# Layer 2's attention: scores ahead of two down products of layer 1, interleaved output products at its end, roots as powers, softmax weights shared by two engines

## The chip, the cores and the metric

The kernel runs on one core of one Trainium2 chip. The metric is the device time of one execution in microseconds (us). Engines: PE (TensorE: matmuls and transposes), DVE (VectorE), ACT (ScalarE), POOL (GpSimd), and SP (SyncE), which only issues DMAs. Each engine runs its instructions in a fixed order; what it needs from another engine it waits for.

## The reference

A model of four layers works on a residual x of 4 x 256 tokens by 256 features. Each layer adds a gated cross-attention over 64 context tokens per batch row, and then a gated feed-forward part; both read the layer-normalised x:

```
for n in 0..3:
    x = x + tanh(g_xattn[n]) * attention_n(layernorm(x), ctx)
    x = x + tanh(g_ffn[n])   * ffn_n(layernorm(x))
layernorm(x) = (x - mean) / sqrt(var + 1e-5)
```

Layers 0 and 1 have a latent attention with 16 heads; layers 2 and 3 a plain one with 16 heads of 16 features and a causal mask (scores = q k / 4, softmax, times v, output product). The feed-forward parts: 0 is a mixture of 16 experts (6 per token) with a shared one, 1 is an MLP 256-1024-256 with weights quantised to -1, 0, 1, 2 is a linear layer with row-wise rounding to 8 bits of both sides, 3 is a mixture of 8 experts (2 per token) with a shared one.

## The kernel before, in words

The 1024 tokens are 8 tiles of 128 (NT = 8), in two groups of four (g = 0, 1; TPG = 4). The residual `x[t]` stays in SBUF. A Python program writes the steps in an order, and a scheduler of the framework orders each engine's instructions from it; `behind(a, b)` adds an edge that keeps a after b on their engines without a wait, `tc.high_priority` pulls a step ahead.

**Softmax attention by tiles.** `in_flight` (L519) runs a pipeline over the tiles: in step i the scores of tile i, the gated add into x of tile i-3, the softmax weights of tile i-1, and `attend` of tile i-2. The scores of a tile go to a `wide` PSUM tile (two exist), DVE takes the row maximum (L1090 in layers 2 and 3, L482 in 0 and 1) and subtracts it (L1092, L483), ACT takes the exponential (L1101, L484). `weights` (L486): DVE sums (L490) and inverts (L491), POOL multiplies all 128x1024 values (L492). `attend` in layers 2 and 3 (L1104): PE transposes the weights (`transposed_pairs`, L506), ACT copies them out of PSUM in two halves (L507), PE multiplies by the values (L1109), ACT copies the context (`ctxTok`, L1118), PE makes the output product (L1121); DVE adds it to x, times the gate (`gated_add`, L517). In layers 0 and 1 `attend` is one product (L714). PSUM has four more `mm` buffers, which all other products share in turn.

**Around layer 2.** `ffn1` (L1886) ends with eight down products (`down`, L1916), each of 24 matmuls on a tile, an addition of the bias and a gated add on DVE. Among the last four stand layer 2's key and value steps (`keys_values`, L1000 and L1016), the layer norm of group 0, its transposes (L461) and its queries (`head_queries`, L476 and L1034). All eight come before the scores of layer 2. Then `used` frees the weight slot of the down products, and SP issues four late loads of layer 3 (L231 and L330).

In layer 2 a side step runs in each step of the pipeline: `queries(1)` (L1043: layer norm of group 1, transposes, queries), and `beside2` (L1130), which makes layer 3's keys and values and at the end calls `rounded(0)` (L1995): layer norm of group 0 for the feed-forward part of layer 2, rounded to whole numbers. `ffn2` (L2016) turns these on PE (L2025), multiplies (L2034), adds (DVE L2038, POOL L2039), rounds group 1, and prepares layer 3's first queries; `kept_busy` (L510) puts matmuls without use there (L512).

**Layer norm** (`layernorm`, L425): DVE's statistics of four tiles (L430, L433), ACT's root (L435, with a load of ACT's table when another function was there), DVE's reciprocal (L438), for the `scalar` form a shift (L442), then four normalised tiles by DVE (L449) or ACT (L446).

Of the kernel before, what the change touches and what calls it, by code (L numbers as in the profile page):

```python
# [30 lines left out]
F32 = mybir.dt.float32  # L31
# [4 lines left out]
AF = mybir.ActivationFunctionType  # L36
# [3 lines left out]
P = 128  # L40
# [57 lines left out]
def tile_flamingo(ctx: ExitStack, tc: tile.TileContext, a: dict, out: bass.AP):  # L98
# [88 lines left out]
    eps = const.tile([P, 1], F32, tag="eps", name="eps")  # L187
    nc.gpsimd.memset(eps, EPS)
    root = small([P, 1], "root", 1)
    nc.scalar.activation(root, eps, AF.Sqrt)  # L190
# [233 lines left out]

    def layernorm(g, scalar=False, after=()):  # L425

        mv = small([P, TPG, 2], "mv")
        for i in range(TPG):
            st = small([P, 6], "st")
            made = nc.vector.bn_stats(st, x[g * TPG + i])  # L430
            if after:
                behind(made, after[0])
            nc.vector.bn_aggr(mv[:, i, :], st)  # L433
        rstd = small([P, TPG], "rstd")
        made = nc.scalar.activation(rstd, mv[:, :, 1], AF.Sqrt, bias=eps)  # L435
        if after:
            behind(made, after[1])
        nc.vector.reciprocal(rstd, rstd)  # L438
        xn = []
        if scalar:  # L440
            shift = small([P, TPG], "shift")
            nc.vector.scalar_tensor_tensor(shift, mv[:, :, 0], -1.0, rstd, ALU.mult, ALU.mult)  # L442
# [42 lines left out]

    def weights(e):  # L486

        groups, n = e.shape[1], e.shape[2]
        sm = sb.tile([P, 16], F32, tag="sm", name="sm", bufs=3)[:, :groups]
        nc.vector.tensor_reduce(sm, e, AX.X, ALU.add)  # L490
        nc.vector.reciprocal(sm, sm)  # L491
        nc.gpsimd.tensor_tensor(e, e, sm.unsqueeze(2).to_broadcast([P, groups, n]), ALU.mult)  # L492

# [24 lines left out]

    def in_flight(scores, attend, gate, beside=iter(())):  # L519

        made, outs = {}, {}
        for i in range(NT + 3):
# [5 lines left out]
            if 1 <= i <= NT:  # L528
                weights(made[i - 1])
            if 2 <= i < NT + 2:  # L530
                outs[i - 2] = attend(i - 2, made.pop(i - 2))

    def paired(steps):
# [143 lines left out]
    def latent_attend(products, wvo, gate, swapped=False, beside=iter(())):  # L677
# [38 lines left out]

        in_flight(scores, attend, gate, beside)

# [318 lines left out]
    def attention23(layer, gate, beside):  # L1037
# [5 lines left out]
        def queries(g):  # L1043

            xn = layernorm(g, layer == 3)
            yield
            xT = transposed(xn)
            yield
            qT.append(head_queries(layer, xT))
# [7 lines left out]
        def scores(t):  # L1057
# [24 lines left out]

            last = side_by_side(lambda half=half, a=a: part(half, a) for half in range(2) for a in range(2))
            if layer == 3 and t == 2:
# [6 lines left out]
            for a in range(2):  # L1091
# [8 lines left out]
                )  # L1100
            nc.scalar.activation(e, e, AF.Exp)  # L1101
            return e

        def attend(t, e):  # L1104
            aT = transposed_pairs(e)
            ps = ps_mm()
# [10 lines left out]
            cT = sb.tile([P, 2 * P], F32, tag="xn", name="ctxTok", bufs=AHEAD + 2)  # L1117
            nc.scalar.copy(cT, ps[:, : 2 * P])  # L1118
            ps = ps_mm()
# [5 lines left out]

        in_flight(scores, attend, gate, zip_longest(queries(1), beside))
        if layer == 3:
            used("L3")

    def beside2(keys):  # L1130
        for i in range(NT + 3):
            if i == NT + 1:
                kept["rounded"] = rounded(0)
            next(keys, None)
            yield
# [750 lines left out]
    def ffn1(gate):  # L1886
# [28 lines left out]

        def down(g, i, terms):  # L1916
            ps = ps_mm()
            for f in range(8):
                for k in range(3):
                    nc.tensor.matmul(  # L1920
                        ps[:, :D],
# [3 lines left out]
                        stop=(f == 7 and k == 2),  # L1925
                    )
            y = sb.tile([P, D], F32, tag="xn", name="y", bufs=AHEAD + 2)
            nc.vector.tensor_tensor(y, ps[:, :D], b2_1, ALU.add)
            gated_add(g * TPG + i, y, gate)

        terms = [up(g) for g in range(NG)]
# [276 lines left out]
```

## Time and profile before

| | us |
|---|---|
| median of 3 runs | 826.48 (822.49 to 829.31) |
| profiled execution, its own time | 826.97 |
| its span in the trace | 825.1 |
| mean granted clock of PE | 0.991 |
| attention of layer 0, 149 to 207: PE busy | 53.91 of 58 |
| attention of layer 1, 420 to 487: PE busy | 64.52 of 67 |
| last up and all down products, 505 to 539: PE busy | 33.95 of 34 |
| attention and feed-forward of layer 2, 539 to 603: PE busy | 55.52 of 64 |
| attention of layer 3, 603 to 653: PE busy | 43.93 of 50 |

All places in time are us from the start of the span. A timeline line has start, length, engine, line, operation, output<-input, shapes and count, and in brackets the idle time of the engine before it with the engine and line that ended it. An fp32 matmul of the program appears as two in the trace. A digit of the page's slices is the busy share in tenths; PEclk is the clock that was granted to PE, 1.00 or 9 being full.

### The profile page before, as it was taken

The numbers are of one execution on the slowest core, as the hardware profiler recorded it, in microseconds if no ns is written. First come the engines' busy times: TensorE is split into PE (matmuls) and PEld (weight loads), VectorE is DVE, ScalarE is ACT, GpSimd is POOL, SyncE is SP. The second block draws the span as 40 slices with busy tenths as digits, with TensorE's granted clock in tenths as the row PEclk, the third lists the DMA queues.
The fourth block names the chain that finished last, engine by engine and source line by source line (L and its number), as shares of the span: only waits on it lengthen the run. The fifth ranks groups of instructions, "written<-read, shape, count | busy, mean of one in ns | idle before, by whom it ended". The sixth has DMA issues, their size and how long they took to land. (4 is left out here: it accounts for less than half of the span.)

```text
span 825.1 us, 12510 instructions
## 1 busy us (share of the span) xinstructions
PE 779.1 (94%) x4509; PEld 523.8 (63%) x4512; DVE 496.2 (60%) x1146; ACT 291.5 (35%) x508; POOL 245.9 (30%) x211
## 2 busy tenths in 40 slices
PE   6999999899999899999999999998898899999994
PEld 4544433777565677766656565755445656999993
DVE  4664455775594455543868759889779564334331
ACT  2221111443421333331643468266455421233320
POOL 0454544232113244322021110024424103444332
PEclk9999999999999999999999999999999999999998
DMA  9510114710021253333840001540000102232211
GB/s 340 198 39 1 39 58 160 274 38 26 26 67 48 63 125 68 73 78 77 296 156 1 8 1 33 191 166 1 26 1 2 52 9 78 53 49 44 29 16 18
DMA packets 32467, 62.44 MB, mean 76 GB/s; under 512 B 5552, under 2 KB 19504, under 8 KB 31696
## 3 DMA queue, kind: packets, MB, share of 16 engines
q1 hardware_dynamic: 25008, 51.91, 18.4%
q0 software_dynamic: 7104, 9.41, 6.8%
q8 instruction: 39, 0.64, 0.3%
q10 hardware_dynamic: 288, 0.26, 0.1%
q14 instruction: 28, 0.23, 0.1%
HBM read 52.81 MB, written 9.27 MB: 75 GB/s over the span
## 5 line engine op out<-in xcount | busy, mean ns | idle before, releaser
L492 POOL TENSOR_TENSOR attn<-attn,sm 128x1024 f32<-128x1024 f32 x32 | 61.1, 1911 | 217.9 <-DVE sm L491 169.1
L476 PE MATMUL wide<-xT,big 128*128 128x512 f32 (+1 forms) x240 | 108.7, 600 | 1.1 <-DVE shared L1678 0.9
L742 DVE TENSOR_TENSOR rope<-wide,big 128x512 f32<-128x512 f32 x96 | 59.6, 682 | 52.1 <-PE wide L476 52.1
L476 PEld LDWEIGHTS wide<-xT,big 128*128 128x128 f32 (+1 forms) x240 | 43.7, 189 | 57.3 <-issue 49.2
L1451 PE MATMUL wide<-blk,still 128*128 128x128 f32 x640 | 74.8, 275 | 0.6 <-DVE blk L1423 0.6
L1451 PEld LDWEIGHTS wide<-blk,still 128*128 128x128 f32 x640 | 73.1, 192 | 0.8 <-issue 0.8
L714 PE MATMUL mm<-vo,attnT 128*128 128x256 f32 x256 | 58.6, 382 | 1.5 <-ACT attnT L507 1.5
L476 PE MATMUL wide<-xT,dense 128*128 128x512 f32 (+1 forms) x120 | 55.1, 599 | 0.0
L714 PEld LDWEIGHTS mm<-vo,attnT 128*128 128x128 f32 x256 | 47.8, 190 | 11.4 <-ACT attnT L507 3.3
L507 ACT COPY attnT<-mm 128x512 f32<-128x512 f32 x64 | 34.6, 587 | 45.6 <-PE mm L506 45.1
L490 DVE TENSOR_REDUCE sm<-attn 128x16 f32<-128x1024 f32 x32 | 38.7, 1208 | 15.2 <-ACT attn L484 13.8
L1413 DVE COPY still<-big 128x1024 f32 x20 | 13.9, 693 | 52.1 <-PE wide L1451 44.7
L1485 POOL DMA_INDIRECT out_dram<-ring,scratch x20 | 31.5, 1577 | 39.3 <-DVE ring L1478 15.7
L1485 POOL DMA_INDIRECT sums<-ring,big x17 | 26.9, 1584 | 48.4 <-ACT ring L1567 18.8
L506 PE MATMUL mm<-ident,attn 128*128 128x128 f32 x256 | 35.4, 284 | 4.5 <-POOL attn L492 4.5
L1469 PE MATMUL mm<-big,hidden 128*128 x160 | 37.8, 380 | 1.4 <-DVE hidden L1462 1.4
L1386 POOL DMA_INDIRECT xs<-xd,scratch x20 | 20.0, 999 | 63.2 <-PE mm L1420 36.7
L506 PEld LDWEIGHTS mm<-ident,attn 128*128 128x128 f32 x256 | 30.6, 146 | 12.6 <-POOL attn L492 7.7
L1461 ACT ACTIVATE hidden<-wide 128x512 f32<-128x512 f32 x20 | 11.9, 597 | 71.2 <-PE wide L1451 66.1
L476 PEld LDWEIGHTS wide<-xT,dense 128*128 128x128 f32 (+1 forms) x120 | 21.5, 185 | 24.4 <-issue 22.0
L517 DVE SCALAR_TENSOR_TENSOR x<-mm,tg,x 128x256 f32<-128x256 f32 x44 | 20.4, 469 | 26.9 <-PE mm L714 15.0
L750 POOL TENSOR_TENSOR rotated<-rope 128x512 f32<-128x512 f32 x12 | 15.3, 1271 | 58.6 <-DVE rope L742 58.6
(363 smaller groups left out, 1572.2 us busy)
## 6 DMA issues: line engine op xcount, KB each, us to landing
big<-in_L_w_gate_up SPq DMA_DIRECT2D x8, 1024.0 KB, 10.4
big<-in_L_w_down SPq DMA_DIRECT2D x8, 512.0 KB, 11.0
w_L_qk<-in_L_qk SPq DMA_DIRECT2D x4, 896.0 KB, 9.5
big<-in_L_w SPq DMA_DIRECT2D x2, 1480.0 KB, 8.1
big<-in_L_w SPq DMA_DIRECT2D x2, 1110.0 KB, 5.2
big<-in_L_wo SPq DMA_DIRECT2D x1, 2048.0 KB, 15.0
big<-in_L_w SPq DMA_DIRECT2D x2, 1024.0 KB, 5.4
xd<-xn SPq DMA_DIRECT2D x16, 128.0 KB, 1.8
```

What stands on the lines that cost most here:

```text
L476: nc.tensor.matmul(ps, w(c), xT[:, c, :], start=(c == 0), stop=(c == 1))
L490: nc.vector.tensor_reduce(sm, e, AX.X, ALU.add)
L492: nc.gpsimd.tensor_tensor(e, e, sm.unsqueeze(2).to_broadcast([P, groups, n]), ALU.mult)
L506: nc.tensor.transpose(ps[:, i * P : (i + 1) * P], ev[:, pr * P : (pr + 1) * P], ident)
L507: nc.scalar.copy(aT[:, half * 4 : half * 4 + 4, :].rearrange("p i t -> p (i t)"), ps)
L517: return nc.vector.scalar_tensor_tensor(x[t], ps, gate, x[t], ALU.mult, ALU.add)
L714: nc.tensor.matmul(ps[:, :D], aT[:, s, :], vo[:, s, :], start=(s == 0), stop=(s == NP - 1))
L742: nc.vector.tensor_tensor(m[:, s, :].rearrange("q (b t) -> q b t", t=S), ps[:, s, :].rearrange("q (b t) -> q b t", t=S), table, ALU.mult,)
L1386: nc.gpsimd.indirect_dma_start(out=xs, out_offset=None, in_=self.xd, in_offset=bass.IndirectOffsetOnAxis(ap=self.gather[:, b : b + 1].bitc ...
L1451: made = nc.tensor.matmul(ps[:, k, f : f + P], w[:, at : at + P], st[:, c * P : (c + 1) * P], start=(c == 0), stop=(c == 1),)
L1469: made = nc.tensor.matmul(ps[:, :D], hT[:, j * P : (j + 1) * P], self.w[:, bass.ds(r + j * D, D)], start=(j == 0), stop=(j == n - 1),)
L1485: nc.gpsimd.indirect_dma_start(out=self.sums[b % len(self.sums)], out_offset=bass.IndirectOffsetOnAxis(ap=self.scatter[:, b : b + 1].bitca ...
```

## The change

1. `ffn1` makes six of its eight down products, then layer 2's first queries. The last two, `down(1, 2)` and `down(1, 3)`, become a generator `down_2`, which stands ahead of `queries(1)` in the side steps of layer 2's pipeline; each of their matmuls is put behind the last scores made so far. With them moves what frees their weights and issues layer 3's late loads.
2. Layers 2 and 3 use `in_flight_parts`: `attend` is cut into transposes, `context` and `output`; for the last tiles the output product of a tile stands after the transposes of the next, and before its values.
3. `layernorm(..., powered=True)` makes 1/root as a power: an addition on DVE and a power (-0.5) on POOL. It is used in layer 2 for group 1's queries and for both groups of `rounded`. `beside2` makes the layer norm one step before the rounding.
4. `weights(e, shared=True)`: DVE multiplies the first eight heads, POOL the last eight. Layers 2 and 3: last tile. Layers 0 and 1: tiles 0, 6 and 7.

```diff
+    power = const.tile([P, 1], F32, tag="power", name="power")
+    nc.gpsimd.memset(power, -0.5)
...
-    def layernorm(g, scalar=False, after=()):
+    def layernorm(g, scalar=False, after=(), powered=False):
...
-        made = nc.scalar.activation(rstd, mv[:, :, 1], AF.Sqrt, bias=eps)
-        if after:
-            behind(made, after[1])
-        nc.vector.reciprocal(rstd, rstd)
+        if powered:
+            nc.vector.tensor_scalar_add(rstd, mv[:, :, 1], EPS)
+            nc.gpsimd.tensor_tensor(rstd, rstd, power.to_broadcast([P, TPG]), ALU.pow)
+        else:
+            made = nc.scalar.activation(rstd, mv[:, :, 1], AF.Sqrt, bias=eps)
+            if after:
+                behind(made, after[1])
+            nc.vector.reciprocal(rstd, rstd)
...
-    def weights(e):
+    def weights(e, shared=False):
...
-        nc.vector.reciprocal(sm, sm)
-        nc.gpsimd.tensor_tensor(e, e, sm.unsqueeze(2).to_broadcast([P, groups, n]), ALU.mult)
+        made = nc.vector.reciprocal(sm, sm)
+        parts = [(nc.vector, slice(0, groups // 2)), (nc.gpsimd, slice(groups // 2, groups))]
+        for engine, part in parts if shared else [(nc.gpsimd, slice(0, groups))]:
+            one = e[:, part]
+            engine.tensor_tensor(one, one, sm[:, part].unsqueeze(2).to_broadcast(list(one.shape)), ALU.mult)
+        return made
...
+    def in_flight_parts(scores, turn, context, output, gate, beside):
+
+        made, ctx, outs = {}, {}, {}
+
+        def add(t):
+            outs[t] = output(ctx.pop(t))
+
+        for i in range(NT + 4):
+            next(beside, None)
+            if i < NT:
+                made[i] = scores(i)
+            if i >= 3 and i - 3 in outs:
+                gated_add(i - 3, outs.pop(i - 3)[:, :D], gate)
+            if 1 <= i <= NT:
+                sums = weights(made[i - 1], shared=i == NT)
+            t = i - 2
+            if 0 <= t < NT:
+                aT = turn(made.pop(t))
+            if t >= NT - 2:
+                add(t - 1)
+                made_x = gated_add(t - 1, outs.pop(t - 1)[:, :D], gate)
+                if t == NT - 2:
+                    behind(made_x, sums)
+            if 0 <= t < NT:
+                ctx[t] = context(t, aT)
+            if 0 <= t < NT - 3:
+                add(t)
+            if t == NT:
+                break
...
-        in_flight(scores, attend, gate, beside)
+        in_flight(scores, attend, gate, beside, shared=(0, NT - 2, NT - 1))
...
-            xn = layernorm(g, layer == 3)
+            xn = layernorm(g, layer == 3, powered=(layer == 2))
...
-        def attend(t, e):
-            aT = transposed_pairs(e)
+        def context(t, aT):
...
-            nc.scalar.copy(cT, ps[:, : 2 * P])
+            made = nc.scalar.copy(cT, ps[:, : 2 * P])
+            if t == NT - 3:
+                behind(made, kept["exp"])
+            return cT
+
+        def output(cT):
...
-        in_flight(scores, attend, gate, zip_longest(queries(1), beside))
+        in_flight_parts(scores, transposed_pairs, context, output, gate, zip_longest(chain(kept.pop("others", ()), queries(1)), beside))
...
+            if i == NT:
+                xn = layernorm(0, True, powered=True)
             if i == NT + 1:
-                kept["rounded"] = rounded(0)
+                kept["rounded"] = rounded(0, xn)
...
+        def down_2():
+            yield
+            down(1, 2, terms[1], kept["scored"])
+            yield
+            down(1, 3, terms[1], kept["scored"])
+            used("L1_w2")
+            load_experts3(EARLY3, E3)
...
         down(1, 0, terms[1])
+        xn = layernorm(0)
         next(keys)
-        xn = layernorm(0)
         down(1, 1, terms[1])
-        next(keys)
-        down(1, 2, terms[1])
+        xT_2 = transposed(xn)
         for _ in range(2):
             next(keys)
-        down(1, 3, terms[1])
-        xT_2 = transposed(xn)
+        kept[2, 0] = head_queries(2, xT_2)
         for _ in keys:
             pass
-        kept[2, 0] = head_queries(2, xT_2)
-        used("L1_w2")
-        load_experts3(EARLY3, E3)
+        kept["others"] = down_2()
...
-    def rounded(g):
+    def rounded(g, xn=None):
...
-        xn = layernorm(g, True)
+        xn = xn or layernorm(g, True, powered=True)
```

More of the change, by code (lines that the diff above doesn't have):

```diff
@@ L517, in gated_add, with in_flight @@
         return nc.vector.scalar_tensor_tensor(x[t], ps, gate, x[t], ALU.mult, ALU.add)
-    def in_flight(scores, attend, gate, beside=iter(())):
+    def in_flight(scores, attend, gate, beside=iter(()), shared=()):
         made, outs = {}, {}
@@ L528, in in_flight @@
             if 1 <= i <= NT:
-                weights(made[i - 1])
+                weights(made[i - 1], shared=i - 1 in shared)
             if 2 <= i < NT + 2:
                 outs[i - 2] = attend(i - 2, made.pop(i - 2))
+    def in_flight_parts(scores, turn, context, output, gate, beside):
[24 more added lines that the diff above has]
+                break
     def paired(steps):
@@ L1081, in part @@
                 )
-            last = side_by_side(lambda half=half, a=a: part(half, a) for half in range(2) for a in range(2))
+            kept["scored"] = last = side_by_side(lambda half=half, a=a: part(half, a) for half in range(2) for a in range(2))
             if layer == 3 and t == 2:
@@ L1100, in scores @@
                 )
-            nc.scalar.activation(e, e, AF.Exp)
+            kept["exp"] = nc.scalar.activation(e, e, AF.Exp)
             return e
-        def attend(t, e):
-            aT = transposed_pairs(e)
+        def context(t, aT):
             ps = ps_mm()
@@ L1914, in up, with down @@
             return hidden[:, g]
-        def down(g, i, terms):
+        def down(g, i, terms, after=None):
             ps = ps_mm()
@@ L1919, in down @@
                 for k in range(3):
-                    nc.tensor.matmul(
+                    made = nc.tensor.matmul(
                         ps[:, :D],
@@ L1926, in down @@
                     )
+                    if after is not None:
+                        behind(made, after)
             y = sb.tile([P, D], F32, tag="xn", name="y", bufs=AHEAD + 2)
```

## The prediction

> **What bounds the kernel now.** I read the page's busy shares first, then stretches of layer 2, then the timelines of PE and DVE there.
>
> ```profile
> PE 779.1 (94%) x4509; PEld 523.8 (63%) x4512; DVE 496.2 (60%) x1146; ACT 291.5 (35%) x508; POOL 245.9 (30%) x211
> ...
> PE   6999999899999899999999999998898899999994
> ...
> PEclk9999999999999999999999999999999999999998
> ```
>
> PE is the bound (94%), so time is won only where PE sits idle or slow. Stretches (columns: length, then busy PE, PEld, DVE, ACT, POOL, granted clock, DMA share):
>
> ```profile
> 523.00:539.00 16.00, 16.00 (x102) 11.02 (x102) 12.67 (x39) 2.62 (x8) 0.00 (x0) 1.00 0.69 244
> 539.00:550.00 11.00, 10.03 (x50) 5.33 (x50) 9.28 (x12) 8.46 (x15) 2.24 (x2) 1.00 0.61 238
> 550.00:560.00 10.00, 9.51 (x84) 5.95 (x82) 9.46 (x15) 5.91 (x11) 3.73 (x3) 1.00 0.01 2
> 560.00:570.00 10.00, 9.43 (x79) 5.89 (x78) 9.69 (x16) 6.29 (x13) 5.34 (x5) 1.00 0.00 0
> 570.00:580.00 10.00, 7.57 (x61) 4.88 (x60) 7.36 (x20) 5.83 (x11) 4.18 (x4) 0.91 0.01 2
> 580.00:590.00 10.00, 7.39 (x67) 5.01 (x66) 6.84 (x23) 5.66 (x12) 2.78 (x4) 0.92 0.06 8
> ```
>
> Until 539 PE is full (down products). From 540 to 570 DVE is full with softmax. From 570 to 588 neither is: PE goes tile by tile through transposes, copy, values, copy, output. PE's timeline of that end, with the idle time before each piece in brackets:
>
> ```profile
> 573.62 1.13 PE L1121 MATMUL mm<-w_L,ctxTok 128*128 128x256 f32 x4 [0.49 <-ACT ctxTok L1118]
> 574.58 1.04 PE L506 MATMUL mm<-ident,attn 128*128 128x128 f32 x8
> 576.65 0.91 PE L1109 MATMUL mm<-attnT,values 128*32 128x128 f32 x16 [1.03 <-ACT attnT L507]
> 578.06 2.02 PE L1121 MATMUL mm<-w_L,ctxTok 128*128 128x256 f32 x4 [0.49 <-ACT ctxTok L1118]
> 579.87 1.86 PE L506 MATMUL mm<-ident,attn 128*128 128x128 f32 x8
> ```
>
> The last two took 2.02 and 1.86 us for 1.13 and 1.04: the granted clock was about half for 3.4 us, after a stretch (574.5 to 578.0) in which PE was busy 1.97 of 3.5 us. Layer 0 shows the same at its first tile, and an idle piece at its last but one:
>
> ```profile
> 155.36 1.97 PE L506 MATMUL mm<-ident,attn 128*128 128x128 f32 x8 [1.65 <-POOL attn L492]
> ...
> 197.62 1.09 PE L506 MATMUL mm<-ident,attn 128*128 128x128 f32 x8 [0.98 <-POOL attn L492]
> ```
>
> DVE's timeline gives its marks; the last line is a 128x4 operation with two SBUF inputs that takes 0.16 us elsewhere and here ends with the POOL weights (576.53 to 578.43):
>
> ```profile
> 540.48 1.22 DVE L1090 TENSOR_REDUCE mx<-wide 128x16 f32<-128x1024 f32 x1 [2.27 <-PE wide L1075]
> ...
> 574.62 1.22 DVE L490 TENSOR_REDUCE sm<-attn 128x16 f32<-128x1024 f32 x1 [1.18 <-ACT attn L1101]
> ...
> 576.65 1.80 DVE L442 SCALAR_TENSOR_TENSOR shift<-mv,rstd 128x4 f32<-128x4 f32 x1
> ```
>
> **The change, part by part.** I placed the new order of each engine by hand, with spacings of the profiled rows: 8 transposes 1.02, scores 1.07, one key half or value step 0.63, head queries 3.63, a down product 2.72, values 0.67 to 0.92, output 1.05; on DVE row maximum 1.15, subtraction 1.20, row sum 1.13, gated add 0.40; on ACT exponential 1.05, two copies 1.05; POOL weights 1.90.
>
> *Scores ahead of the down products.* Both orders agree to 526.27. Then: transposes 1.0, key half 0.6, value 0.55, head queries 3.63, three values 1.6, scores 1.07, in all 8.5: scores of tile 0 are done at 534.75 (before: 540.4). The two moved products (5.44 of PE, the same work) now cover the softmax of tiles 0 and 1. Gain for DVE at this place: 5.7.
>
> *What is late next.* Group 1's queries need the last down product, now done at 541.85 (before 533.4). Behind it stand on DVE its addition, a sum and a maximum; then the new root and xn, done at 549.05 (before 538.2). On PE, transposes of xn and tile 1, its values and output stand ahead of the head queries, and wait for copies (0.85, 1.2): queries 555.65 to 559.3, scores of tile 4 at 561.0 (before 557.75). DVE, 5.7 ahead at the start, stands idle 4.0 there. From that maximum on it has 15.4 left to the last row sum, which starts at 576.5, 1.9 later than before. The early start by itself buys nothing at this point.
>
> *Interleaved products.* The tail was not bound by that sum: its weights were ready at 578.43 and used at 584.30. In the new order transposes of tile 6 wait for their weights (576.1 to 578.0), then output 5, values 6, transposes 7, output 6, values 7, output 7: 1.0 + 1.05 + 0.65 + 1.0 + 0.55 (copy behind the four xn on ACT) + 1.05 + 0.65 + 0.45 + 1.05 = 7.45, so 585.5 instead of 588.35. The copies' waits (0.49 twice, 0.3 to 0.4 twice) lie under other products and the 1.7 of slow clock and the table load (1.28 on ACT, 0.7 of PE's 1.03) fall away. Through layer 2's feed-forward the chain last gated add, statistics, shift follows: shift at 589.1 instead of 592.21. Gain 3.0; ends 0 (queries 3 later still) and 5.7 (DVE keeps its lead). The four y there (1.66 on DVE) hide its power. Two order-only edges (context copy 5 behind the last exponential, gated add 5 behind the last row sum's reciprocal) are in these times: the copy is ready 2 us after that exponential, and nothing but statistics follows the add.
>
> *Roots as powers.* Three times a 128x4 addition on DVE (0.2) and a power on POOL replace root (0.30), reciprocal (0.18) and one table load. No row shows a power. Ends: 0.19 (a 128x8 cast on POOL) and 1.90 (POOL's weights); I take 0.5, near the small row. It stands ahead of POOL's weights of tiles 1 and 7, and DVE's xn waits for it; both are in the times above. The constant -0.5 is one memset of 0.09 beside the first loads: nothing.
>
> *Weights shared.* Half on POOL: 1.05 (between 0.40 for 128x128 and 1.91 for 128x1024); half on DVE: 0.69 (128x512 from SBUF twice). If they overlap, a tile's weights are 0.85 shorter; if they exclude each other, 0.17. The 1.80 above, and another 128x512 operation of 1.73 instead of 0.48 beside POOL's weights at 452, speak for exclusion; subtraction from PSUM beside POOL keeps its 1.28. The Trainium skill, SBUF — State Buffer, "Who interferes with whom", states it: a DVE instruction with two SBUF inputs contends with a GpSimd one that reads SBUF, and the loser blocks. By that rule the sum stands as below; by free overlap it would be 1.4 lower. I take exclusion. It counts where PE waits for POOL: layer 0, tiles 0 and 6 (2 x 0.15), plus 0.46 of layer 0's scores that now stand ahead of tile 0's transposes in that idle time: 0.8. Ends: 0 (DVE's copy delayed by 0.7 to 1.2, covered by its own wait of 1.51 at 159.45) and 3.2 (overlap twice, and no slow clock at 155.36). Layer 1: PE waited 0.30 there; its DVE halves lie before waits of 2.5: 0 (ends -0.3 and 0.3). Layer 2 and 3's tile 7: not waited for.
>
> *Layer 3.* Same interleaving: outputs 5 and 6 lose 0.49 each, values 6 and 7 0.29 each, less 0.3 for tile 6's weights (POOL 641.82 to 643.72): gain 1.2 (ends 0.3, 1.6).
>
> *Queues.* SP issues the four last loads (533.51 on) some 8 us later; they land in about 10 and are first read at 653: nothing.
>
> Sum: 0.8 + 3.0 + 1.2 = 5.0. Profiled execution 826.97 (span 825.1): 822.0; it stands 0.5 over the median 826.48, so **821.5**.
>
> **The rivals.**
> - *Clock falls at group 1's queries.* In my placing PE is busy about 1.7 of 3.5 us before them; 1.97 of 3.5 was followed by half clock, 2.65 (571.0 to 574.5) was not. 3.4 us at half clock cost 1.7: 823.2. Against it: three estimated waits make that idle. The Trainium skill, TensorE: Matmul & The Clock Gate, Part 1, ties the drop to an idle window of about 3.4 us; by it there would be none. The trace dropped after gaps of only 1.03 and 1.65.
> - *Overlap and kept clock in layer 0.* Gain there 3.2 instead of 0.8, and up to 2 us less waiting at the queries: 816 to 819. For it: POOL's row alone sets T0's wait. Against it: the 1.80.
> - *The late queries take everything.* Layer 2's gain 0 if they come 3 us later still: 824.5.
> - *Slower: the power is slow.* With a price p it delays xn of group 1 and, ahead of tile 7's weights, the tail (0.25 of slack): loss 2p - 1.2. At 1.9 us: 824; from 3.1 us the change is slower than before, at 5 us 830. No POOL row that computes is over 1.9, but none is a power.
>
> **How the numbers follow.** Forecast 0.45, clock falls 0.17, overlap 0.25, late queries 0.08, slow power 0.05. A measurement of this kernel tells about 1% (8.3 us) from none: faster by over 1% is below 818.2. That holds 0.18 of the overlap case and 0.07 of the forecast's edge: 0.25. Slower by over 1% (834.7): half of the slow power and a little, 0.04. Rest 0.71. The range 815.5 to 827 leaves out 0.1 below and 0.1 above.
>
> **What would show it.** Scores of tile 0 about 5.5 us earlier than before; DVE idle some 4 us ahead of tile 4's maximum; the last output 2 to 4 us earlier, with no wait for the context copy before outputs 5 and 6; the power below 1 us; DVE's half of the weights starting when POOL's ends. I am wrong if the power is over 2 us, if DVE does not stand at tile 4, or if PE's clock falls in a new place.

## The result, and the profile after

The changed kernel takes 827.86 us (median, 825.13 to 831.33) beside 825.3 (822.32 to 829.31) before: a ratio of 1.004, 95% interval 1.0025 to 1.0055. It is 0.4% slower, about 2.6 us, where 5 us less was forecast. The profiled execution took 827.87 (span 826.0). A second measurement of the same kernel, later, gave 827.23 and a ratio of 1.0024 (1.0005 to 1.0043).

The first lines of the page, as shown of before:

```profile
PE 777.5 (94%) x4509; PEld 523.2 (63%) x4512; DVE 505.3 (61%) x1154; ACT 290.8 (35%) x505; POOL 244.0 (30%) x215
...
PEclk9999999999999999999999999999999999999998
```

The shares tell nothing; only DVE has 9 us more work. The stretches of layer 2 (length, busy PE, PEld, DVE, ACT, POOL, granted clock, DMA share, GB/s):

```profile
539.00:550.00 11.00, 8.03 (x66) 5.18 (x64) 10.47 (x15) 4.10 (x9) 4.65 (x3) 1.00 0.77 267
550.00:560.00 10.00, 8.15 (x44) 5.15 (x45) 9.23 (x19) 4.44 (x8) 2.58 (x3) 0.83 0.34 127
560.00:570.00 10.00, 10.00 (x67) 5.80 (x66) 6.19 (x9) 4.14 (x9) 1.41 (x1) 1.00 0.00 0
570.00:580.00 10.00, 8.19 (x72) 5.17 (x70) 8.91 (x17) 7.21 (x14) 4.18 (x6) 1.00 0.01 2
580.00:590.00 10.00, 7.49 (x83) 5.25 (x84) 8.79 (x30) 5.84 (x13) 6.65 (x7) 1.00 0.01 2
```

From 539 to 560 PE is busy 16.18 us of 21, where it was 19.54, and from 550 to 560 its clock was 0.83, not 1.00. From 560 to 570 DVE is busy 6.19 of 10 us, where it was full. The clock of 0.91 and 0.92 that was granted from 570 to 590 is gone. PE's timeline there, with idle time in brackets:

```profile
547.32 1.13 PE L1165 MATMUL mm<-w_L,ctxTok 128*128 128x256 f32 x4 [0.49 <-ACT ctxTok L1157]
550.49 1.64 PE L467 MATMUL mm<-ident,xn 128*128 128x128 f32 x8 [2.04 <-DVE xn L455]
...
553.61 1.94 PE L516 MATMUL mm<-ident,attn 128*128 128x128 f32 x8 [0.86 <-ACT xT L169]
...
558.52 3.60 PE L482 MATMUL mm<-xT,w_L 128*128 128x512 f32 x8
...
581.90 1.09 PE L516 MATMUL mm<-ident,attn 128*128 128x128 f32 x8 [0.70 <-POOL attn L501]
```

The transposes of group 1's xn wait 2.04 us and again inside (1.64 for 1.02, since xn is done at 551.3); tile 1's wait 0.86 and then run at about half clock (1.94 for 1.09), which lasts from 553.1 to 556.5. The queries are at 558.52. Before, they and the scores of tile 4, the first that need them, were here:

```profile
542.87 3.70 PE L476 MATMUL mm<-xT,w_L 128*128 128x512 f32 x8
...
552.92 1.14 PE L1075 MATMUL wide<-kbd,xT 64*128 64x256 f32 x8
```

DVE's timeline shows why xn was late:

```profile
542.28 2.04 DVE L527 SCALAR_TENSOR_TENSOR x<-y,tg,x 128x256 f32<-128x256 f32 x1
...
548.34 2.97 DVE L455 TENSOR_SCALAR xn<-x,mv,rstd 128x256 f32<-128x256 f32 x4 [0.46 <-POOL rstd L439]
...
563.66 1.22 DVE L1130 TENSOR_REDUCE mx<-wide 128x16 f32<-128x1024 f32 x1 [3.73 <-PE wide L1115]
...
580.07 1.20 DVE L496 TENSOR_REDUCE sm<-attn 128x16 f32<-128x1024 f32 x1
```

And POOL's, in the same stretch:

```profile
542.14 1.90 POOL L501 TENSOR_TENSOR attn<-attn,sm 128x1024 f32<-128x1024 f32 x1 [63.08 <-DVE sm L497]
547.26 1.05 POOL L439 TENSOR_TENSOR rstd<-rstd,power 128x4 f32<-128x4 f32 x1 [3.21 <-DVE rstd L438]
548.29 1.89 POOL L501 TENSOR_TENSOR attn<-attn,sm 128x1024 f32<-128x1024 f32 x1
```

Before, the same two operations of DVE ran while POOL had nothing to do (547.76 is its first weight product there):

```profile
533.97 0.48 DVE L517 SCALAR_TENSOR_TENSOR x<-y,tg,x 128x256 f32<-128x256 f32 x1
...
536.82 1.38 DVE L449 TENSOR_SCALAR xn<-x,mv,rstd 128x256 f32<-128x256 f32 x4
```

In the changed kernel the addition of the last product begins 0.14 after POOL's weights and ends 0.28 after them; xn begins with the next weights and ends 1.1 after them. The Trainium skill, SBUF — State Buffer, "Who interferes with whom", says that a DVE instruction with two SBUF inputs (the addition) contends with a GpSimd one that reads SBUF, and that a `tensor_scalar` (xn) can contend too; the 2.04 and 2.97 agree.

**One stage after the other.** The table has the length of each stretch of the profile, minus that of before (us, from PE's timelines). Ffn is a layer's feed-forward part. "First transposes" are those of tile 0's softmax weights; "layer 2, tail" is from these to the last output. A row is one execution: e1's was the slowest of its twelve, e2's the fastest. The time ahead of layer 0's softmax part is not in the table; it is 0.8 to 3.7 us shorter in these four executions than in that of before.

| kernel | layer 0, softmax part | layer 0's ffn | layer 1, attention | its ffn, to layer 2's first transposes | layer 2, tail | ffn behind it | layer 3, tail | last ffn |
|---|---|---|---|---|---|---|---|---|
| changed | -1.46 | +1.13 | +0.92 | -5.35 | +7.06 | +1.18 | -1.23 | -0.83 |
| interleaved products only (e1) | -1.39 | -0.04 | 0.00 | 0.00 | -2.17 | +1.77 | -1.23 | -0.82 |
| products put back (e2) | -1.47 | -0.10 | +0.90 | +0.01 | -3.29 | 0.00 | -1.24 | +0.09 |
| moved products only (e5) | -1.39 | -0.14 | -0.01 | -5.35 | +7.59 | +1.55 | -0.01 | +1.67 |

A granted clock of about half for 3.4 us, a clock fall from here on, takes 1.70 to 1.71 us of clock each time. In time it costs less where PE waits anyway: 1.4 us for the fall at 154 (first column), 0.8 for the one at 660 (last column). Such falls are in all these profiles: before at 154, 578 and 660 us, changed at 269, 553 and 600, e1 at 582 and 596, e2 at 651, e5 at 547, 598 and twice from 660 on. All have another 2.3 to 3.4 us of lost clock at the end of the span, behind PE's last product, where it costs nothing. The clock of the timed runs is recorded too, so the mean span can be cut in two: what the clock took at most (span times one minus the mean granted clock), and the rest.

| kernel | median us | ratio to before (95%) | mean clock | mean span | clock took at most | rest |
|---|---|---|---|---|---|---|
| before (beside e1, e2) | 825.08 | | 0.9909 | 823.0 | 7.5 | 815.5 |
| changed | 827.86 | 1.004 (1.0025 to 1.0055) | 0.9885 | 826.5 | 9.5 | 817.0 |
| e1, interleaved products only | 820.54 | 0.9941 (0.9921 to 0.9961) | 0.9938 | 818.6 | 5.1 | 813.5 |
| e2, products put back | 819.64 | 0.994 (0.9919 to 0.9961) | 0.9950 | 818.2 | 4.1 | 814.1 |
| e5, moved products only | 829.51 | 1.0062 (1.0039 to 1.0085) | 0.9889 | 827.9 | 9.2 | 818.7 |

### The profile page after: what moved, and what is told of

It is laid out like the page before. It is cut to its first block, busy times and chain, and to the rows that moved or that the text cites. A ratio compares the mean times of both kernels' runs of the same rounds, so it can differ in the third digit from the quotient of the medians.

```text
span 826.0 us, 12522 instructions
## 1 busy us (share of the span) xinstructions
PE 777.5 (94%) x4509; PEld 523.2 (63%) x4512; DVE 505.3 (61%) x1154; ACT 290.8 (35%) x505; POOL 244.0 (30%) x215
## 5 line engine op out<-in xcount | busy, mean ns | idle before, releaser
L501 POOL TENSOR_TENSOR attn<-attn,sm 128x1024 f32<-128x1024 f32 (+1 forms) x32 | 56.0, 1750 | 226.9 <-DVE sm L497 182.3
L1507 ACT ACTIVATE hidden<-wide 128x512 f32<-128x512 f32 x20 | 11.9, 597 | 71.2 <-PE wide L1497 65.7
L836 ACT COPY big<-mm 128x512 f32<-128x512 f32 x16 | 8.6, 589 | 67.9 <-PE mm L824 61.7
```

Source lines behind the costliest of these rows:

```text
L501: engine.tensor_tensor(one, one, sm[:, part].unsqueeze(2).to_broadcast(list(one.shape)), ALU.mult)
```

## The experiments

The theories: A, group 1's queries wait for the moved products and come late. B, the shared weights cost it. C, what a stage wins is given back by clock falls in the next. D, the power on POOL is too slow. E, the loss is clock falls alone.

**e1, the interleaved products alone.** The two down products, layer norms and `weights` as before; `in_flight_parts` kept (`others` is empty here).

```diff
-        in_flight(scores, attend, gate, zip_longest(queries(1), beside))
+        in_flight_parts(scores, transposed_pairs, context, output, gate, zip_longest(chain(kept.pop("others", ()), queries(1)), beside))
```

> Before, with only the interleaved products in the ends of layers 2 and 3 (down products in their old place, roots as before, POOL alone multiplies the weights). Theory A (the moved down products spoil group 1's queries of layer 2; the rest of the change is sound): layer 3's attention about 1.2 us shorter than before, layer 2's 1 to 2 us, since its last products no longer wait for the context copies; in all 2 to 3 us faster than before, 822.5 to 823.5 beside 825.3. Theory B (the shared weights of layers 0 and 1 cost it): the same 2 to 3 us here, so this run alone does not part A from B. Theory C (what a stage wins is given back by clock falls in the stage after it): at most 0.5 us faster than before, 825.

Measured: 820.54, 4.5 us less than before, more than A or B gave it. C falls, although the profiled execution, the slowest, gives 1.77 back in the ffn behind layer 2, with a fall at 596. Layer 3 gives the 1.23 forecast. By the second table at most 2.4 of the 4.5 is clock and 2.0 the rest.

**e2, the changed kernel with the products put back.**

```diff
+        down(1, 2, terms[1])
...
+        down(1, 3, terms[1])
...
-        kept["others"] = down_2()
```

> The changed kernel with layer 1's last two down products put back into their feed-forward; everything else of the change is kept. Theory A: group 1's queries of layer 2 are at about 543 again (558.5 in the changed kernel), VectorE does not stand idle 3.7 us at tile 4's row maximum, layer 2's attention ends 2 to 4 us earlier: 823 to 825, so 3 to 5 us faster than the changed kernel's 827.9. Theory B (shared weights): 827 to 828, as the changed kernel. Theory C: layer 2 ends earlier and the feed-forward behind it gives half of it back: 826.

Measured: 819.64, 8.2 us less than the changed kernel. The moved products cost all of the loss and hide a gain of 5.4. DVE's first row maximum and last row sum of layer 2 in e2:

```profile
536.16 1.22 DVE L1130 TENSOR_REDUCE mx<-wide 128x16 f32<-128x1024 f32 x1 [1.48 <-PE wide L1115]
...
570.31 1.22 DVE L496 TENSOR_REDUCE sm<-attn 128x16 f32<-128x1024 f32 x1 [0.99 <-ACT attn L1141]
```

That is 34.15 us from one to the other; before it is 34.14 (540.48 to 574.62), in the changed kernel 46.02 (534.05 to 580.07). In e2, as before, PE makes group 1's queries while tile 0's softmax runs:

```profile
538.56 3.70 PE L482 MATMUL mm<-xT,w_L 128*128 128x512 f32 x8
```

**e4, without shared weights in layers 0 and 1.**

```diff
-        in_flight(scores, attend, gate, beside, shared=(0, NT - 2, NT - 1))
+        in_flight(scores, attend, gate, beside)
```

> The changed kernel, but in layers 0 and 1 POOL alone multiplies all weights. Theory A: the shared weights gain in layer 0 what they lose at the end of layer 1: 827 to 828.5, as the changed kernel. Theory B: layer 1's end is 1.4 us shorter and the feed-forward of layer 0 no longer has its slow products (1.1 us): 825 to 826, 2 to 3 us faster than the changed kernel.

Measured: 828.13, ratio 1.0033 (1.0009 to 1.0058), as the changed kernel; B falls as the cause. Its profile shows a small cost all the same. Layer 1's attention is 0.90 to 0.92 longer than before in eleven profiles with shared weights (a twelfth, e14's, has a clock fall there), and within 0.02 of before in all four of my kernels without. Where it comes from, on PE in the changed kernel:

```profile
476.92 0.63 PE L516 MATMUL mm<-ident,attn 128*128 128x128 f32 x4 [1.20 <-DVE x L527]
```

and on DVE:

```profile
475.69 0.69 DVE L501 TENSOR_TENSOR attn<-attn,sm 128x512 f32<-128x512 f32 x1
476.30 0.48 DVE L527 SCALAR_TENSOR_TENSOR x<-mm,tg,x 128x256 f32<-128x256 f32 x1
```

DVE's half of tile 7's weights stands ahead of a gated addition; the second half of tile 6's transposes waits for that addition, which is the last reader of an accumulator. In e4 these transposes do not wait.

**e5, the moved products alone**, in the kernel before.

```diff
-        in_flight(scores, attend, gate, zip_longest(queries(1), beside))
+        in_flight(scores, attend, gate, zip_longest(chain(kept.pop("others", ()), queries(1)), beside))
```

> Before, with only the two down products moved behind layer 2's first scores (old order of the ends, roots by the activation engine, POOL alone multiplies the weights). Theory A: the first scores come 6 us earlier and buy nothing; group 1's queries come 13 to 16 us later than before (556 to 559 beside 542.87), VectorE stands idle 3 to 4 us at tile 4, and layer 2's attention ends 1 to 4 us later than before: 827 to 829.5. Theory B: the moved products are harmless: 823 to 825.5. If the power on POOL is what makes them late (rival D), the queries come at 556 here and the time is 825 to 826.

Measured: 829.51, 4.4 us slower than before, as A says; queries at 555.27, 14.3 behind the first transposes (changed: 14.4), a pause of 3.78 at tile 4. There is no power in this kernel: D falls.

**e3, the changed kernel without powers.**

```diff
-            xn = layernorm(g, layer == 3, powered=(layer == 2))
+            xn = layernorm(g, layer == 3)
```

(and the same at the two other places)

> The changed kernel with roots by the activation engine and reciprocals in place of the three powers. Theory D (the power, 1.05 us on POOL, is what makes group 1's queries late): queries 1 us earlier and 1 to 2 us less time. Theory A: the two table loads that return on the activation engine (1.28 us each) and the reciprocal make up for it: 827 to 829, as the changed kernel's 827.9.

Measured: 827.30, ratio 1.0035 (1.001 to 1.006), beside 827.23 for the changed kernel on the same chip. The powers neither gain nor lose.

**e10, products put back and no shared weights in layers 0 and 1**: the edits of e2 and e4.

> The changed kernel with the two down products back in their feed-forward and without shared weights in layers 0 and 1: what is left is the interleaved products, the roots as powers in layer 2 and the shared last tile in layers 2 and 3. The end of layer 1 was 0.9 us longer in both profiles with shared weights than in the three without, and layer 0's attention equal within 0.1; by that 818.5 to 819, 0.9 us below the kernel with the down products back (819.64). If the shared weights earn in layer 0 what I took (0.8): 819.5 to 820.

Measured: 821.72 beside 826.22 of before, ratio 0.9944 (0.9922 to 0.9967). It cannot be told from e1 (0.9941) or e2 (0.994). The 0.9 us of the profiles is too little for such a measurement.

**e13, queries that do not wait for the moved products.** Group 1's queries are made from x without the last two products in tiles 6 and 7, so they are emitted behind group 0's, ahead of the first scores. This leaves those products out of the queries, so the kernel does not compute the model's result; it serves to measure time alone.

```diff
-        in_flight_parts(scores, transposed_pairs, context, output, gate, zip_longest(chain(kept.pop("others", ()), queries(1)), beside))
+        in_flight_parts(scores, transposed_pairs, context, output, gate, zip_longest(kept.pop("others") if layer == 2 else queries(1), beside))
...
+        xn = layernorm(1)
         for _ in range(2):
             next(keys)
         kept[2, 0] = head_queries(2, xT_2)
+        kept[2, 1] = head_queries(2, transposed(xn))
```

> The changed kernel with group 1's queries of layer 2 made right behind group 0's, ahead of the first scores: they read x before the last two down products are added to tiles 6 and 7, which leaves those products out of the queries of these tiles (they are still added to x). So the moved products and the early scores stay, and the late queries go. Theory A (moving is harmful because the queries wait for the moved products): VectorE has no pause before tile 4's row maximum; from the first row maximum to the last row sum 34.1 us as before, plus 2.7 for the two additions with statistics and 1.6 if one still stands beside POOL's weights, from a start 5.4 us earlier: the last row sum 1 to 2.5 us earlier than with the products in their old place, time 817.5 to 819, so about 9 us under the changed kernel. Theory E (the clock falls come whenever the scores stand ahead of the products): 823 or more.

Measured: 819.28 beside 824.61 of before, ratio 0.9926 (0.9898 to 0.9955), clock 0.9947, and no slow stretch in the profile but the one at its end. The products are still behind the scores; the dependence is gone, and with it the whole loss. So the moved products do their harm by way of group 1's queries, as A says. Its size is not parted by e13: with the dependence went the wait, but also xn with its exclusion, the statistics and the power out of the softmax stretch, and the clock falls. DVE's first row maximum and last row sum here:

```profile
531.02 1.23 DVE L1132 TENSOR_REDUCE mx<-wide 128x16 f32<-128x1024 f32 x1 [0.54 <-PE wide L1117]
...
571.66 1.22 DVE L496 TENSOR_REDUCE sm<-attn 128x16 f32<-128x1024 f32 x1 [0.99 <-ACT attn L1143]
```

They are 40.64 apart, not the 38.4 that I had expected. PE is busy 38.46 us of these 40.64, and DVE waits for it. So the early start is nearly used up even here; the time is about that of e2.

**e6, the bias early**, which takes the two-SBUF-input additions off the chain.

```diff
+        for t in (NT - 2, NT - 1):
+            gated_add(t, b2_1, gate)
...
+            if after is not None:
+                gated_add(g * TPG + i, ps[:, :D], gate)
+                return
```

> The changed kernel, but the bias of tiles 6 and 7 goes into x ahead of their down products (twice a gated addition of 0.48 us on VectorE while POOL is idle), so that the additions of the two moved products read PSUM and SBUF instead of SBUF twice. Theory A (the moved products are late because two-SBUF-input work stands beside POOL's weights): the gated addition of the last product takes 0.5 us instead of 2.04, the addition of the bias (0.4) is gone from the chain, xn of group 1 and the queries come about 2 us earlier, the pause of 3.7 us before tile 4's row maximum falls to about 1.7, and the time from 827.9 to 825 to 826. Theory E (the loss is in clock falls alone, and those come from the idle pieces of PE, wherever VectorE's work stands): below 1 us gained. Theory D (the power is what makes the queries late): below 1 us.

**e7, the same, and tile 1's weights wait for xn.**

```diff
+            if after is not None:
+                apart(mul, after)
```

> As the run with the early bias, and POOL's weights of layer 2's tile 1 also wait until VectorE has written xn of group 1, so that these four operations run alone. Theory A: xn takes 1.4 us instead of 2.97, queries another 1.6 us earlier, hardly a pause before tile 4's row maximum; tile 1's transposes, which stand behind those of xn on PE, hardly wait; 823 to 824.5. Theory E: as the run before it, or later by the wait of tile 1's weights (up to 1.5 us).

Measured: 828.07, ratio 1.0025 (1.0003 to 1.0048), and 827.18, ratio 1.0032 (1.0008 to 1.0055), beside 826.22 of before: no gain that can be told. In e6 the exclusions are gone from the addition and from xn already, so that e7 has nothing left to add. DVE in e6:

```profile
540.12 0.39 DVE L527 SCALAR_TENSOR_TENSOR x<-mm,tg,x 128x256 f32<-128x256 f32 x1
...
543.47 1.38 DVE L455 TENSOR_SCALAR xn<-x,mv,rstd 128x256 f32<-128x256 f32 x4
```

Yet its queries stand 14.3 behind the first transposes (14.0 in e7), about as before the edit, since something else stands ahead of the transposes of xn:

```profile
547.36 0.60 PE L1105 MATMUL wide<-causal,ident 128*128 128x512 bf16 x2 [2.30 <-DVE attn L1132]
```

The scheduler has put xn ahead of tile 2's softmax on DVE, and tile 4's mask product ahead of tile 0's output on PE; that product needs the buffer which tile 2's subtraction frees.

**e15, the same with the mask product held back** behind the transposes of xn.

```diff
+                    if layer == 2 and t == TPG:
+                        behind(made, kept["turned"])
```

> As the run with the early bias, with one order-only edge more: the mask product of tile 4 stands behind the transposes of xn on PE again, as in the changed kernel (in the run with the early bias it had moved ahead of them, and PE stood 2.30 us in it, for a subtraction). So the port exclusions go and nothing takes their place ahead of the transposes. Theory A1 (the exclusions of 1.6 and 1.6 us make the queries late): queries 12 to 13 us behind the first transposes of layer 2 (14.4 in the changed kernel), the pause at tile 4 under 2.5 us, 825 to 826.5. Theory F (the queries are late by their place on PE, behind tile 1's transposes, values and output with two copies each): transposes of xn earlier, queries where they were, 827 to 828.5.

Measured: 828.30, ratio 1.0048 (1.0026 to 1.0069); no gain. PE now stands at tile 0's output:

```profile
548.91 2.07 PE L1167 MATMUL mm<-w_L,ctxTok 128*128 128x256 f32 x4 [3.64 <-ACT ctxTok L1159]
```

and ACT shows what its copy stood behind, the exponential of tile 2, which waited for DVE:

```profile
547.54 1.06 ACT L1143 ACTIVATE attn<-attn 128x1024 f32<-128x1024 f32 x1 [3.24 <-DVE attn L1134]
548.50 0.35 ACT L1159 COPY ctxTok<-mm 128x256 f32<-128x256 f32 x1
```

Theory A1, that the exclusions make the queries late, does not hold by itself: without them DVE's full queue holds PE at another place for as long.

**e16, queries ahead of tile 1 on PE.**

```diff
             xT = transposed(xn)
-            yield
+            if layer != 2:
+                yield
             qT.append(head_queries(layer, xT))
```

> The changed kernel with group 1's queries emitted one step sooner, right behind the transposes of xn, so that tile 1's transposes, values and output stand behind them on PE. Theory F: queries 10 to 12 us behind layer 2's first transposes (14.4 in the changed kernel), pause at tile 4 under 1.5 us, last row sum 2 to 3 us earlier, 823 to 825.5, more if the clock falls go with the idle pieces. Theory A1: the transposes of xn are as late as before (6.4 us behind the first transposes) and PE then waits for their copies; at most 1 us gained, 826.5 to 828.

**e17, e15 and e16 together.**

> Early bias, mask product held and queries ahead of tile 1 together: the best that I can make of the moved products while the result stays the same. If the lateness of the queries is all that is wrong with them (as the run with queries ahead of the last products says: 819.3), the pause at tile 4 goes and the time is 820 to 823, at or a little above the kernel with the products in their old place (819.6); if VectorE's extra work in the softmax stretch counts for itself: 823 to 826.

Measured: 827.29, ratio 1.0024 (1.0005 to 1.0043), and 826.11, ratio 1.0019 (1.0002 to 1.0037), beside 825.40 of before. The queries come 9.4 and 10.0 behind the first transposes, 4.4 to 5 us sooner than in the changed kernel, but the pause at tile 4 is still 3.39 and 4.34, and the last row sum stands 35.6 and 36.6 behind the first transposes (changed: 36.0). Both clock falls are there in e17, two in a row at the queries in e16. F, the place on PE, accounts for 0 to 2 us. With the result kept, no order that I tried with the moved products is faster than before.

**e9 and e12, PE kept busy** by four and by two products that nobody reads, between tile 0's output and the transposes of xn.

```diff
+            if layer == 2 and g == 1:
+                kept_busy(4, ps_mm(), kept["made_out"])
             xT = transposed(xn)
```

> The changed kernel with four products more, whose result nobody reads, on PE between the output of layer 2's tile 0 and the transposes of xn, about 1.8 us in the 2.0 us in which PE waited there. Theory A (late queries cost by the wait): not faster, 827.5 to 829. Theory E (half of the loss or more is a clock fall that follows this gap): the mean granted clock rises from 0.9885 by 0.002 to 0.004 and the time falls by 1.7 to 3.4 us, to 824.5 to 826.

> The changed kernel with two such unread products instead of four: four ran for 3.60 us (0.9 each) in a gap of 2.0 us and put the queries 1.3 us later. Two take 1.8. Theory E (a clock fall follows the gap and part of the loss is its): mean granted clock 0.990 or more beside 0.9885, no slow stretch between 545 and 565 us nor in the feed-forward behind it, queries not later than in the changed kernel, and 1.7 to 3.4 us less time: 824.5 to 826.5. Theory A (the late queries themselves): 827 to 829.

Measured: 830.07, ratio 1.0054 (1.0026 to 1.0082), and 828.99, ratio 1.0043 (1.002 to 1.0066). The four took 3.60 us and put the queries 1.3 later; the mean clock rose to 0.9907 (at most 7.7 us taken instead of 9.5), but the rest grew from 817.0 to 820.4. The profile has no fall before its end, but it is of an execution with a clock of 0.997, the highest of the nine. The two took 1.88; PE then waited 1.35 further on and the clock fell as before (0.9887). So filling costs more than it saves. E, by which the falls alone are the loss, does not hold by the second table: the changed kernel's rest too is 2.9 longer than in e2. That the falls follow the idle pieces is not shown by these two runs.

**e14, the changed kernel once more.**

> The changed kernel itself once more, for a second profile and times beside the three others. Theory E: slow stretches of PE at group 1's queries (about 9 us behind the first transposes of layer 2) and in the feed-forward behind layer 2 are found again, since the idle pieces that lead to them are the same in each execution; 827.5 to 828.5. If the falls are chance alone, the slow stretches of this profile lie elsewhere.

Measured: 827.23. Its stretches around the queries and in the feed-forward behind:

```profile
550.00:555.00 5.00, 2.97 (x11) 1.98 (x10) 4.92 (x7) 1.32 (x2) 1.93 (x2) 0.68 0.92 360
555.00:560.00 5.00, 4.50 (x30) 2.78 (x29) 4.48 (x8) 3.23 (x7) 1.26 (x1) 0.64 0.05 18
...
601.00:606.00 5.00, 4.03 (x15) 2.21 (x16) 2.83 (x10) 3.03 (x6) 1.99 (x3) 0.70 0.01 3
```

Both falls are found again (3.41 us lost at the queries, in two stretches on end, and 1.70 behind layer 2), and one at 459 that was not there before. Over all profiles: with queries that wait for the moved products the clock fell at them in all but one (e9), the changed kernel's two profiles among them; without (before, e1, e2, e10, e13) in none of five. In the feed-forward behind layer 2 it fell in ten of twelve (not in e9 and e16), and in one of those five (e1). These two falls go with the late queries; the falls at 154 (before), 269 (changed, e7, e10, e12) and around 655 (before, e2, e5) come and go between executions.

## Why the prediction was wrong, point by point

The forecast was 5 us of gain; the measured change is 2.6 us of loss. For the profiled execution it was 822.0, and that took 827.87. Of these 5.9 us, 4.7 lie in layer 2 up to its last output (1.7 longer for my 3.0 shorter), 1.2 in the ffn behind it, 0.9 in layer 1's attention and 1.1 in layer 0's ffn (the fall at 269, which comes and goes); other places give about 2 back. What came out by its own steps:

- **Scores ahead of the down products: the step as a move was right, its price wrong.** The first scores are 5.4 us earlier against the same base (first transposes -5.35; forecast 5.7 for DVE). What I held to be paid for them, 1.9 us at the last row sum, is 5.7: the changed kernel's first row maximum is 6.2 earlier than before, measured from the end of layer 1's attention, and the way from there to the last row sum 11.9 longer. That way is 11.9 longer by: 4.5 of moved work (two y, each a product plus its bias, 0.79; two additions 0.96; statistics 1.2; xn 1.38; epsilon 0.16), 3.2 of exclusion beside POOL (2.04 - 0.48 and 2.97 - 1.38) and 4.1 more of idle time (the waits in brackets, 6.10 for 1.99). My placing made it 41.75 (534.75 to 576.5); it is 46.02. Of the 4.3 missing, 3.4 lie ahead of tile 4's maximum; behind it DVE took 16.4 for my 15.4, with a wait of 1.09 that I had put at nothing.
- **"What is late next": the step that failed.** From the end of the last down product to the end of xn I took 7.2 us (541.85 to 549.05); it was 10.4 (540.93 to 551.31). The 3.2 between them are what the two exclusions cost: I had let the addition and xn take the time of undisturbed rows, though I had read the exclusion from the 1.80 and used it for the shared weights. So xn was done at 551.3 for 549.05, queries at 558.52 for 555.65, tile 4's maximum at 563.66 for 561.0; the pause of 4.0 is 3.73. I also misread how late that is: the 557.75 that I gave for tile 4's scores before is tile 5's, and tile 4's were done at 554.0, so its maximum comes 7.8 us later (563.66 for 555.85), not the 3.25 that my numbers made of its scores. But e6 and e15 show that this is not all: with the exclusions gone PE waits as long, at the mask product (2.30) or at an output (3.64), for the softmax of tile 2. The lasting fault is that I followed one chain through a stretch in which DVE has no room. Before, PE makes the queries (3.70) and their transposes in the shadow of tile 0's softmax, that is, while it would wait for DVE, ACT and POOL anyway. The change puts the down products (5.44) into the same shadow, and queries, transposes and 4.5 us of DVE's work behind it. e13, where the queries stay in the shadow, loses nothing.
- **Rival: clock falls at group 1's queries.** I gave it 0.17 and one fall of 1.7, and named a fall in a new place as a sign of being wrong. It came, with a second fall behind layer 2; by the mean clocks the moved products cost at most 5.4 of their 8.2 us in clock (9.5 against 4.1) and at least 2.9 in the rest. The two are not parted: e9 saved 1.8 of clock with filling and lost 3.4 in the rest. How the clock's part is divided among places is not settled, since the profile shows one execution only.
- **Interleaved products: right in layer 3, hidden in layer 2.** Layer 3's tail is 1.23 to 1.25 shorter in all fifteen profiles with it (forecast 1.2) and 0.01 in e5 without. Alone it is worth 4.5 us (e1). With the moved products in their old place layer 2's tail is 2.17 shorter in e1, with a fall in it, and 3.29 in e2 and e10. In layer 2 it could not show in the changed kernel, where the row sum came last: I had added its gain to a row sum that was itself later. From tile 6's transposes to the last output it took 7.9 us for my 7.45; output 6 still waited 0.61 for its context copy.
- **Slow clock taken as a property of the code.** The falls at the transposes of 155.36 and 579.87 in the one profile that I had took 1.7 of clock each. The first comes and goes: layer 0's softmax is 1.39 shorter in the four kernels that leave it alone. The second is gone in e2, e10 and e13, but my sum was made against an execution that had both. So most of layer 0's 1.46 in the changed kernel is luck, and the 0.8 forecast there did not come.
- **Weights shared.** The exclusion was rightly taken: DVE's half takes 1.54 beside POOL's 1.04 (layer 2 of e2 has 1.53). Layer 0: 0.08 for my 0.8. Layer 1: 0.9 of loss in the profile for my 0 (ends 0.3), by the delayed addition; too small for the timed runs (e4, e10).
- **Roots as powers.** 1.05, 1.01 and 1.02 us for my 0.5, between the ends. In time nothing that these runs can tell (e3), and e5 loses 4.4 without any power, so the rival of a slow power falls: by its own formula, 2p - 1.2, p = 1.05 would have cost 0.9. (One row of POOL was longer than the 1.9 that I held for the longest: 2.22 at 451.20.)
- **Queues.** SP's late loads: nothing, as said; the last ffn is 0.8 shorter, not longer, in all kernels but e2 and e5. These two have a fall around 655, as before has, so the 0.8 is the missing fall and no gain.
- **Layer 2's ffn taken to pass everything on.** Its 1.18 us more are the second clock fall: e16, which lacks it, is as long there as before, within 0.02.

The kernels with the products in their old place (e1 with the interleaved products alone, e2 and e10 with more of the change: ratios of 0.994) are the ones to keep; which of the three is best is below what these runs can tell.

## What to carry to other kernels

When a block of work is moved ahead of another on a full engine, ask what stood in its shadow until now and where that goes: here 5.4 us of early start were paid for with queries and additions put into a stretch in which DVE had no room. A dependence of the next group on the moved work must be followed through every in-order queue on its way, and rows that run beside POOL's SBUF work be priced with the exclusion. One profile's slow clock is one execution's: count it only over many runs, and look for new falls wherever a change leaves PE half idle for some microseconds: eleven of the twelve profiles with late queries have one there.

## What the runs showed of the hardware that I had not expected

- The clock falls come in pieces of about 1.7 us of lost clock (half clock for 3.4 us), and two or three can follow each other (3.41 in e14 and e16, 5.12 over 11 us in e4). No busy share of PE parts the places where they come. In the 5 us ahead of the fall at the queries PE was busy 1.57 (e15) to 3.33 (e12); e9 had 2.80 of 5 there, and e2, e10 and e13 2.98 of 5 between 587 and 598, without a fall; and ahead of the falls at 660 (before) and 651 (e2) PE was busy all 5 us. The Trainium skill, TensorE: Matmul & The Clock Gate, Part 1, ties the fall to an idle window of about 3.4 us. In e15 and e17 there is an idle piece of that length (3.64 and 3.65), but in e5 the longest ahead of the fall is 0.94, so the fall comes without one too, and the measurement decides. That page also says that the window runs free of the kernel; the places that come and go between executions of one kernel agree with that.
- Between 35 executions of the kernel before the mean clock goes from 0.986 to 0.997, and the time follows it (correlation -0.87).
- The addition of epsilon, a 128x4 operation of 0.16 us on DVE with one SBUF input and constants, took 1.07 beside POOL's weights in e6 and ended with them (542.30 and 542.28), as if it were excluded too.
- A power of 128x4 on POOL takes 1.01 to 1.05 us, as long as its weights for 128x512 (1.04).
